# One GpSimd instruction of the front moved: the BatchNorm power behind the second norm shift

## The chip, the cores and the metric

The kernel runs on one core of one Trainium2 chip. The metric is the device time of one execution in microseconds. A core has five engines that run their own instruction streams in program order and wait for each other by semaphores: TensorE (PE, matmul), VectorE (DVE), ScalarE (ACT), GpSimd (POOL) and SyncE (SP, which here only issues DMAs).

## The reference, cut to what matters

The input x has 8 images of 512 channels and 32 x 32 points, all in float32. One block is computed:

- a GroupNorm of x with 32 groups of 16 channels each (mean and variance over the 16 channels and all points, then (x - mean) / sqrt(var + 1e-5));
- cv1, a 1x1 convolution 512 to 512, then BatchNorm with given statistics and SiLU; its output is cut into two halves of 256 channels, y0 and y1;
- two bottlenecks in a row on y1, each a 3x3 convolution with BatchNorm and SiLU, an attention of 4 heads over the 1024 points, a 1x1 convolution with BatchNorm and SiLU, and a residual;
- cv2, a 1x1 convolution over the 1024 channels of y0, y1 and the two bottleneck outputs, with BatchNorm and SiLU, added to x.

What the change touches is the front of this:

```python
x = x + layer(gn(x))                          # gn: GroupNorm
s = g / jnp.sqrt(v + BN_EPS)                  # BatchNorm factor of every convolution
cbs = silu((conv(x, w) - m) * s + b)          # conv, BatchNorm, SiLU
```

## The kernel before, in words

The eight images are worked off in four pairs. Before the first pair stands a front, in which everything that later stages take for granted is made for the first time: the images are loaded, the filters of the 3x3 convolution are transformed (`make_u`, on DVE with a few copies on ACT), the BatchNorm factors of all layers are made, image 0 and image 1 are normalised, and cv1 is computed for both. From about 78 us on PE works on the 3x3 convolution of the first pair.

An image is four tiles of 128 channels by 1024 points (`x` for image 0, `x_second` for image 1). The GroupNorm of some of these tiles is `group_norm_part` (L820). Its steps are:

- statistics per channel, on DVE (L770, L771) or, for tiles named in `by_act`, on ACT (L811 to L818);
- means over the groups by a small matmul with a constant matrix (`gm_ps`, L777), then the deviations on DVE (L786 to L789: `gm` is the negative mean, `dev` the variance), then a second small matmul (`gv_ps`, L777) and `gr = gv_ps + eps` on DVE (L796);
- on POOL `gr = gr ** -0.5` (L797) and `shift = gm * gr` (L833);
- on ACT `x = gr * x + shift`, half a tile at a time (L839).

Image 0 is done in two parts: its tiles 0 and 1 first, its tiles 2 and 3 as a second part of the same function. Image 1 is a third call, with all four tiles.

The BatchNorm factors need `rstd = (var + eps) ** -0.5` for 16 columns: `nc.vector.tensor_scalar` adds the epsilon (L2131), POOL takes the power (L2132), and later DVE makes the scale `sh` and the bias `bh` out of it (L2139 to L2144). They are read first by the first SiLU of cv1 (L523, on ACT).

cv1 of an image is, for each of 4 output tiles, a sum over 4 input tiles (k) and 2 halves. A float32 matmul of 512 columns shows as two rows in the trace. In the front the sums are begun with the tiles that are normalised first: before the second norm part is there, PE works on k = 0 and 1 of three output tiles (`begin`, 24 rows); then it goes on with k = 2 and 3 (L551, 32 rows), until the small matmul `gm_ps` of image 1 stands in its stream; then half an output tile, `gv_ps`, the last half, and then image 1 (64 rows).

The order on each engine is the order in which the tile scheduler emits instructions. `tc.issue_after(ins)` puts an instruction behind another one in that order; engines wait only for what they read or overwrite. POOL issues DMAs too: the stores of the transformed filters (L481) stand in the same stream behind the shifts.

Of the kernel before, what the change touches and what calls it, by code (L numbers as in the profile page):

```python
# [62 lines left out]
def kernel(  # L63
# [1965 lines left out]
    s = stages(act, small, ps_big, ps_av, 6)  # L2029
# [71 lines left out]
    with tc.issue_after(loaded.ins), tc.issue_after(averaged.ins):  # L2101
        for _ in range(5):
            made = next(chunk)
# [17 lines left out]
    with tc.issue_after(averaged.ins):  # L2121
        made = next(chunk)
# [3 lines left out]
    with tc.issue_after(first.ins), tc.issue_after(made.ins):  # L2126
        multiplied, _, applied, powered = next(norm)
    with tc.issue_after(multiplied.ins):
        begin(Y_ORDER[2], range(NX // 2))
    with tc.issue_after(made.ins), tc.issue_after(powered.ins):  # L2130
        nc.vector.tensor_scalar(rstd, bnp[:, :, 3], BN_EPS, None, ALU.add)  # L2131
        scaled = nc.gpsimd.tensor_tensor(rstd, rstd, mhalf[:, :NBN], ALU.pow)  # L2132
        for _ in range(4):
            made = next(chunk)
    with tc.issue_after(made.ins):
# [2 lines left out]
    with tc.issue_after(made.ins):  # L2138
# [4 lines left out]
        for at in bn_m1:  # L2143
            made = nc.vector.tensor_scalar(sh[:, at : at + NM], sh[:, at : at + NM], 1 / 36, None, ALU.mult)  # L2144
# [17 lines left out]
    with tc.issue_after(made.ins):  # L2162
        for _ in range(2):
            made = next(chunk)
# [3 lines left out]
    for steps, times in ((other, 2), (chunk, 3)):  # L2168
        with tc.issue_after(made.ins):
            for _ in range(times):  # L2170
                made = next(steps)
# [10 lines left out]
    multiplied, read, applied, powered = second["norm"]  # L2182
    shifted = s.shift_made[0]
    copies_behind[0] = applied
    with tc.issue_after(read.ins):
        for _ in range(2):
            made = next(chunk)
# [777 lines left out]
```

## Time and profile before

| what | value |
|---|---|
| time, median of 3 runs | 2205.9 us (2205.38 to 2206.28) |
| the profiled execution's own time | 2206.06 us |
| its span, first to last instruction | 2204.5 us |
| mean granted TensorE clock | 0.998 of full speed |
| PE busy | 2176.4 us, 99% of the span |
| DVE busy | 1814.6 us, 82% |
| ACT busy | 1094.6 us, 50% |
| POOL busy | 216.9 us, 10% |

A row of the timeline gives the start, the time from there to the end of the last instruction in it, the engine, the line, what is written from what, how many instructions are merged in it, and in brackets how long the engine had sat idle before it and what ended that. Matmul ends are modelled. A row of a waits view gives who waited for whom, the total, how often, and the longest. A row of a windows view gives a stretch, its length, the busy time of each engine with its count of instructions, the granted clock and the DMA load.

### The profile page before, as it was taken

The page shows a single profiled execution, that of the slowest core. Times are in us where ns is not written, and L with a number is a line of the kernel's source. Part 1 is how long each engine was busy: PE and PEld are TensorE (multiplying, and loading weights), DVE is VectorE, ACT ScalarE, POOL GpSimd, SP SyncE. Part 2 cuts the span into 40 slices and gives each one's busy share as a digit, 9 for nine tenths or more (in the row PEclk, how much of TensorE's full clock was granted, in tenths as well). Part 3 has the DMA queues.
Part 4 walks back from the last instruction along what each step waited for, and adds up shares of the span by engine and source line. Part 5 has one row for each costly group of instructions (what it writes and reads, how often), then busy time and mean ns, then how long its engine had stood idle before and what let it go on. Part 6 is the DMA issues. An engine that isn't in the chain of part 4 may idle for free.

```text
span 2204.5 us, 41005 instructions
## 1 busy us (share of the span) xinstructions
PE 2176.4 (99%) x16546; PEld 1121.3 (51%) x16546; DVE 1814.6 (82%) x3002; ACT 1094.6 (50%) x1320; POOL 216.9 (10%) x387
## 2 busy tenths in 40 slices
PE   7999999999999999999999999999999999999998
PEld 3653437343484444734458443564346734383445
DVE  7988879878978688986898868997798877897676
ACT  6555553554225666356314676456522465336543
POOL 3322210000210000000022000000002100000001
PEclk9999999999999999999999999999999999999999
DMA  6954547212583323612159141543126811261224
GB/s 220 338 173 130 181 132 279 83 49 78 143 284 107 104 99 120 214 50 77 56 137 328 35 161 42 180 144 103 33 68 176 295 30 45 92 207 36 68 59 116
DMA packets 133129, 290.75 MB, mean 132 GB/s; under 512 B 33636, under 2 KB 58976, under 8 KB 131908
## 3 DMA queue, kind: packets, MB, share of 16 engines
q1 hardware_dynamic: 101908, 200.62, 27.5%
q0 software_dynamic: 31024, 87.44, 13.2%
q8 instruction: 132, 2.16, 0.4%
q14 instruction: 65, 0.53, 0.1%
HBM read 218.40 MB, written 69.60 MB: 131 GB/s over the span
## 4 chain that ended last, share of the span: by engine, by line
PE 95%; DVE 3%; issue 1%; DMA 1%; ACT 0%; SPq 0%; POOL 0%; DVEq 0%; ACTq 0%; POOLq 0%
PE av_ps L1138 19%; PE l_ps L1101 19%; PE c_ps L689 11%; PE p_ps L975 8%; PE c L1375 6%; PE m_ps L1355 5%; PE ps L551 5%; PE c_q L1423 5%; PE x_ps L1847 4%; PE p_ps L981 3%; PE c L1407 3%; PE c_new L1375 2%; PE s_ps L1156 1%; DVE acc L1122 1%; PE p_ps L937 1%
## 5 line engine op out<-in xcount | busy, mean ns | idle before, releaser
L1105 ACT ACTIVATE pt<-l_ps 128x1024 f32<-128x1024 f32 x512 | 495.9, 1023 | 332.5 <-PE l_ps L1101 256.1
L1138 PE MATMUL av_ps<-pt,vT 64*64 64x512 f32 x4096 | 484.9, 590 | 0.8 <-DVE z L1146 0.8
L1101 PE MATMUL l_ps<-q,kr 64*64 64x512 f32 x4096 | 485.2, 590 | 0.0
L1122 DVE TENSOR_TENSOR acc<-acc,pt 128x1024 f32<-128x1024 f32 x362 | 442.8, 1223 | 37.2 <-ACT pt L1105 9.4
L1138 PEld LDWEIGHTS av_ps<-pt,vT 64*64 64x64 f32 x4096 | 157.5, 133 | 278.3 <-issue 234.5
L1101 PEld LDWEIGHTS l_ps<-q,kr 64*64 64x64 f32 x4096 | 158.4, 133 | 267.9 <-issue 245.2
L689 PE MATMUL c_ps<-v_in,u 128*64 128x128 f32 x4320 | 238.4, 273 | 0.3
L689 PEld LDWEIGHTS c_ps<-v_in,u 128*64 128x64 f32 x4320 | 235.7, 137 | 5.2 <-issue 5.2
L1146 DVE TENSOR_TENSOR z<-av_ps,z 128x512 f32<-128x512 f32 x64 | 44.0, 688 | 97.5 <-ACT z L1145 97.3
L1355 PE MATMUL m_ps<-z,m_sb 128*128 128x512 f32 x256 | 114.1, 593 | 0.0
L975 PE MATMUL p_ps<-t_z,sq 128*128 128x512 f32 x224 | 105.9, 595 | 0.0
L694 ACT COPY c_m<-c_ps 128x512 f32<-128x512 f32 x48 | 28.1, 585 | 150.5 <-PE c_ps L689 131.5
L1119 DVE TENSOR_TENSOR acc<-pt 128x1024 f32<-128x1024 f32 x64 | 78.1, 1221 | 14.2 <-PE s_ps L1156 9.2
L523 ACT ACTIVATE t<-m_ps,bh,sh 128x512 f32<-128x512 f32 x64 | 46.3, 773 | 86.5 <-PE m_ps L1355 85.3
L975 PE MATMUL p_ps<-z,sq 128*128 128x512 f32 x168 | 81.3, 604 | 0.2
L1355 PEld LDWEIGHTS m_ps<-z,m_sb 128*128 128x128 f32 x256 | 47.7, 190 | 56.8 <-issue 51.4
L1523 POOL DMA_DIRECT2D c_out<-in_x_dram x48 | 43.5, 1049 | 294.7 <-ACT c_out L523 292.1
L1214 DVE TENSOR_TENSOR z<-z,rs 128x512 f32<-128x512 f32 x64 | 42.4, 687 | 33.3 <-DMA rs<-r_dram 33.2
L523 ACT ACTIVATE z<-z,bh,sh 128x512 f32<-128x512 f32 x64 | 48.8, 811 | 22.9 <-DVE z L754 22.9
L975 PEld LDWEIGHTS p_ps<-t_z,sq 128*128 128x128 f32 x224 | 39.5, 191 | 36.5 <-issue 34.4
L523 ACT ACTIVATE c_out<-c,bh,sh 128x512 f32<-128x512 f32 x12 | 14.0, 1278 | 85.7 <-PE c L1407 77.7
L1847 PE MATMUL x_ps<-t_x,sw 128*128 128x512 f32 x128 | 55.9, 592 | 0.0
(410 smaller groups left out, 3342.0 us busy)
## 6 DMA issues: line engine op xcount, KB each, us to landing
u<-u SPq DMA_DIRECT2D x135, 512.0 KB
y_in<-y SPq DMA_DIRECT2D x32, 512.0 KB
rs<-r_dram SPq DMA_DIRECT2D x126, 128.0 KB
sq<-sq SPq DMA_DIRECT2D x42, 384.0 KB
x<-in_x_dram SPq DMA_DIRECT2D x28, 512.0 KB
r_in<-r SPq DMA_DIRECT2D x28, 512.0 KB
c_out<-in_x_dram POOLq DMA_DIRECT2D x56, 256.0 KB, 6.6
out_dram<-c_out POOLq DMA_DIRECT2D x56, 256.0 KB, 5.2
```

Of the source, the lines that this page charges most:

```text
L523: silued[0] = nc.scalar.activation(dst, src, AF.Silu, scale=sh[:, k : k + 1], bias=bh[:, k : k + 1])
L551: last_product[0] = nc.tensor.matmul(ps[:, half, :], w_of(k), rhs_of(k, half), start=(k == begin), stop=(k == end))
L689: conv_product[0] = nc.tensor.matmul(to[o], us[cp][:, k, row, c, o], rhs, start=(k == 0), stop=(k == NM - 1),)
L975: nc.tensor.matmul(ps[:, o, :], w[:, o, :], rhs, start=not onto, stop=True, skip_group_check=onto)
L1101: nc.tensor.matmul(ps[kh * HD : (kh + 1) * HD, hd, :], kr[r, c, o : o + HD], q[r, c, ts(half, HALF)], start=True, stop=True,)
L1105: last_exp[0] = exp = nc.scalar.activation(pt, ps, AF.Exp, scale=SCALE)
L1122: ins = nc.vector.tensor_tensor(accs[g], accs[g], pt[i], ALU.add)
L1138: nc.tensor.matmul(avs[g][hd * HD : (hd + 1) * HD, kh, :], vT[r, j, o : o + HD], pt[i][r, hd, :], start=(j == 0), stop=(j == NJ - 1),)
L1355: nc.tensor.matmul(pss[half][:, oc, :], m2_sb[:, n, k, ts(oc, P)], ao[:, k, ts(half, HALF)], start=(k == 0), stop=(k == NM - 1),)
L1375: nc.tensor.matmul(ps[:, o, :], w[:, k, ts(o, P)], rhs[part][:, c], start=(k == 0 and not onto), stop=(k == KB - 1), skip_group_check=onto,)
L1423: nc.tensor.matmul(to, a[:, c], b[:, c], start=first and c == 0, stop=last and c == 1, skip_group_check=True)
L1847: nc.tensor.matmul(ps[:, o, :], w[:, c, ts(o, P)], rhs[c], start=(c == 0 and not onto), stop=(c == 1), skip_group_check=onto,)
```

## The change

The power of the BatchNorm factors is one POOL instruction of 128 x 16 elements. Before, it was ordered behind `powered`, the power of the second norm part of image 0, and so came between that power and the shift that is made from it. Now it is ordered behind that shift. Nothing else is changed; what is computed is the same.

```diff
     with tc.issue_after(made.ins), tc.issue_after(powered.ins):
         nc.vector.tensor_scalar(rstd, bnp[:, :, 3], BN_EPS, None, ALU.add)
+    with tc.issue_after(made.ins), tc.issue_after(s.shift_made[0].ins):
         scaled = nc.gpsimd.tensor_tensor(rstd, rstd, mhalf[:, :NBN], ALU.pow)
+    with tc.issue_after(made.ins), tc.issue_after(powered.ins):
         for _ in range(4):
             made = next(chunk)
```

Three instructions in a row on POOL, in the front: the power `gr_331` and the shift `shift_334` of the second norm part of image 0, and the power `rstd_135` of the BatchNorm factors. Before:

```order
L797 TENSOR_TENSOR gr_241<-gr_241,mhalf_126 128x2
L833 TENSOR_TENSOR shift_244<-gm_232,gr_241 128x2
L797 TENSOR_TENSOR gr_331<-gr_331,mhalf_126 128x2
L2132 TENSOR_TENSOR rstd_135<-rstd_135,mhalf_126 128x16
L833 TENSOR_TENSOR shift_334<-gm_310,gr_331 128x2
L481 DMA u0120_151<-u_new_408 128x512
L481 DMA u0121_152<-u_new_408 128x512
```

With the change, at the same place (its line is now L2133):

```order
L797 TENSOR_TENSOR gr_241<-gr_241,mhalf_126 128x2
L833 TENSOR_TENSOR shift_244<-gm_232,gr_241 128x2
L797 TENSOR_TENSOR gr_331<-gr_331,mhalf_126 128x2
L833 TENSOR_TENSOR shift_334<-gm_310,gr_331 128x2
L2133 TENSOR_TENSOR rstd_135<-rstd_135,mhalf_126 128x16
L481 DMA u0120_151<-u_new_408 128x512
L481 DMA u0121_152<-u_new_408 128x512
```

The power of 16 columns and the shift of 2 columns have changed places; the stores of the filters follow as before. On PE, DVE, ACT and SP no instruction stands at another place.

## The prediction

> **What bounds the kernel now.** I read the page first, then the waits of PE, then the timelines of the engines in the front.
>
> ```profile
> span 2204.5 us, 41005 instructions
> PE 2176.4 (99%) x16546; PEld 1121.3 (51%) x16546; DVE 1814.6 (82%) x3002; ACT 1094.6 (50%) x1320; POOL 216.9 (10%) x387
> PE ps L551 <- ACT x L839: 5.8, 2, 3.1
> PE ps L551 <- ACT x_second L839: 0.9, 1, 0.9
> ```
>
> PE is busy 99% of the span. What delays it can be counted on one hand, and a good part stands in the front: matmuls of cv1 (L551) that wait for ACT to normalise their input (L839), once 3.1 us, once 0.9. The timeline of PE gives the places.
>
> ```profile
> 22.18 3.70 PE L551 MATMUL ps<-x,w_cols 128*128 128x512 f32 x8
> 29.03 15.70 PE L551 MATMUL ps<-x,w_cols 128*128 128x512 f32 x32 [3.15 <-ACT x L839]
> 44.66 0.28 PE L777 MATMUL gm_ps<-mv,gmat 64*64 64x4 f32 x4
> 44.87 1.98 PE L551 MATMUL ps<-x,w_cols 128*128 128x512 f32 x4
> 46.78 0.28 PE L777 MATMUL gv_ps<-dev,gmat 64*64 64x4 f32 x4
> 46.99 1.98 PE L551 MATMUL ps<-x,w_cols 128*128 128x512 f32 x4
> 49.83 27.73 PE L551 MATMUL ps<-x_second,w_cols 128*128 128x512 f32 x64 [0.85 <-ACT x_second L839]
> ```
>
> PE stands still from 25.88 to 29.03. The 64 rows at 49.83 take 27.73 us, 0.433 us each; the 32 at 29.03 take 15.63 to the next start instead of 13.9. The granted clock says why:
>
> ```profile
> 30.40:33.80 3.40, 3.40 (x6) 1.30 (x4) 3.33 (x14) 3.40 (x6) 0.00 (x0) 0.51 0.02 8
> 33.80:36.00 2.20, 2.20 (x7) 1.00 (x6) 2.20 (x7) 2.17 (x7) 1.08 (x2) 0.99 0.22 88
> ```
>
> For 3.4 us after the pause PE runs at 0.51 of its clock, which costs about 1.7 us more. What ACT waits for stands on POOL:
>
> ```profile
> 9.93 0.83 POOL L797 TENSOR_TENSOR gr<-gr,mhalf 128x2 f32<-128x2 f32 x1 [7.04 <-DVE gr L796]
> 10.84 0.54 POOL L833 TENSOR_TENSOR shift<-gm,gr 128x2 f32<-128x2 f32 x1
> 22.54 0.70 POOL L797 TENSOR_TENSOR gr<-gr,mhalf 128x2 f32<-128x2 f32 x1 [11.16 <-DVE gr L796]
> 23.20 3.12 POOL L2132 TENSOR_TENSOR rstd<-rstd,mhalf 128x16 f32<-128x16 f32 x1
> 26.29 1.84 POOL L833 TENSOR_TENSOR shift<-gm,gr 128x2 f32<-128x2 f32 x1
> 28.07 0.74 POOL L481 DMA_DIRECT2D u<-u_new  x1
> 48.71 0.22 POOL L833 TENSOR_TENSOR shift<-gm,gr 128x4 f32<-128x4 f32 x1
> 11.41 2.93 ACT L839 ACTIVATE x<-x,shift,gr 128x512 f32<-128x512 f32 x4 [1.97 <-POOL shift L833]
> 28.16 2.93 ACT L839 ACTIVATE x<-x,shift,gr 128x512 f32<-128x512 f32 x4 [5.60 <-POOL shift L833]
> ```
>
> The first norm part of image 0 goes from the start of its power (9.93) to ACT (11.41) in 1.48 us. The second takes 5.62 (22.54 to 28.16), because the 16-column power lies between.
>
> **Step 1, ACT and the pause of PE.** Power and shift now follow each other as in the first part: ACT starts at 22.54 + 1.48 = 24.02, 4.14 us earlier. PE had its first matmul 0.87 us after ACT's start (29.03 less 28.16), so the data is there at 24.89, before PE is done with its 24 earlier rows at 25.88. ACT makes half a tile in 0.73 us (2.93 / 4), PE uses it in two rows, 0.87 us, so PE never catches up. The pause of 3.15 us goes, and with it what called up the low clock. The 32 rows end at 25.88 + 32 x 0.433 = 39.75, and `gm_ps` of image 1 could start there, 4.9 us earlier than 44.66.
>
> **Step 2, what is late next.** `gm_ps` also needs ACT's statistics of image 1, and behind it stands DVE.
>
> ```profile
> 31.00 1.04 ACT L811 ACTIVATE junk<-x_second 128x1024 f32<-128x1024 f32 x1
> 36.01 2.26 ACT L523 ACTIVATE ypad<-ps,bh,sh 128x512 f32<-128x512 f32 x2
> 42.68 0.21 ACT L818 ACTIVATE mv<-square 128x4 f32<-128x4 f32 x1
> 45.40 1.21 ACT L523 ACTIVATE y_half<-ps,bh,sh 128x512 f32<-128x512 f32 x1
> 48.96 2.93 ACT L839 ACTIVATE x_second<-x_second,shift,gr 128x512 f32<-128x512 f32 x4 [2.35 <-POOL shift L833]
> 26.59 0.28 DVE L447 TENSOR_SCALAR u_new<-ypad 128x256 f32<-128x256 f32 x1
> 31.19 0.18 DVE L2139 TENSOR_TENSOR sh<-bnp,rstd 128x16 f32<-128x16 f32 x1
> 31.72 0.23 DVE L2144 TENSOR_SCALAR sh<-sh 128x2 f32<-128x2 f32 x2
> 41.23 0.43 DVE L464 SCALAR_TENSOR_TENSOR u_new<-taps,u_new 128x256 f32<-128x256 f32 x1
> 44.98 0.16 DVE L786 TENSOR_SCALAR gm<-gm_ps 128x4 f32<-128x4 f32 x1 [3.33 <-PE gm_ps L777]
> 45.71 0.16 DVE L789 TENSOR_TENSOR dev<-dev,mv 128x4 f32<-128x4 f32 x1
> 47.11 0.16 DVE L796 TENSOR_SCALAR gr<-gv_ps 128x4 f32<-128x4 f32 x1 [0.76 <-PE gv_ps L777]
> DVE gm L786 <- PE gm_ps L777: 3.3, 1, 3.3
> DVE gr L796 <- PE gv_ps L777: 1.9, 2, 1.1
> ```
>
> ACT works without a gap from 28.16 to the end of its statistics at 42.89. Moved by 4.14 us, the first SiLU (36.01) comes to 31.87, where its `sh` is ready at 31.95 (end of L2144); a tenth is lost, and the statistics end at about 38.9, before PE needs them at 39.75.
>
> DVE does not move. From 22.30 on it transforms filters without a gap, until 41.66 (41.23 + 0.43), and only then reads `gm_ps`, in program order. In the trace it waits there 3.33 us and again 0.76 for `gv_ps`; the last two rows, the waits of DVE from 20 to 100 us, hold no other wait after that. So DVE can get nearer by 3.33 + 0.76 = 4.09 us and no more. Does it get all? `gm` starts at 41.65. `dev` ends 0.89 later (45.71 + 0.16 less 44.98), at 42.54. PE has by then done `gm_ps` and the 4 rows behind it (39.75 + 0.21 + 1.73 = 41.7), so `gv_ps` starts at about 42.7 and `gr` 0.33 later (47.11 less 46.78), at 43.02 instead of 47.11. That is all of it.
>
> **Step 3, from there on.** Power and shift of image 1 and ACT's L839 follow `gr` by the same times as before: ACT at 44.87 instead of 48.96 (the SiLU row at 45.40, ended at 46.61 before, ends at about 42.5), PE on image 1 at 45.74 instead of 49.83. PE is short of work for about 1.0 us before `gv_ps` and 1.1 before image 1, but these lie inside the 4.09. From 49.83 on PE is full, and DVE too: both streams move as they are. Later loads and stores are started by the same engines, so they move along.
>
> **Step 4, the instruction that is moved.** The 16-column power now starts at about 24 and ends 3.12 later at 27.1; if the shift's 1.84 us before was its tail (the shifts at 10.84 and 48.71 took 0.54 and 0.22), 1.3 to 1.6 later. DVE asks for it at 31.19, so at least 2.4 us cover it. The store L481, and what follows it on POOL, waits only for finished ACT work and moves from 28.07 to about 27.1.
>
> ```profile
> 24.00:26.00 2.00, 1.88 (x5) 0.57 (x3) 2.00 (x6) 0.00 (x0) 2.00 (x1) 1.00 1.03 408
> 28.00:30.00 2.00, 0.97 (x3) 0.49 (x4) 1.93 (x6) 1.84 (x3) 0.81 (x2) 1.00 1.16 348
> 30.00:32.00 2.00, 2.00 (x4) 0.81 (x3) 1.93 (x10) 2.00 (x4) 0.00 (x0) 0.61 0.17 63
> ```
>
> The DMA engines are full until 30 and then empty, so all tiles of image 1 are there by 30. ACT now asks for the first at 26.95 (24.02 + 2.93) rather than at 31.00. In the worst case it waits until 30, gains only 1.0, and the statistics end at 41.9: `gm` comes at 42.2, and 3.5 us of the gain are left. At 408 GB/s a tile of 512 KB takes 1.3 us and they come in order, ahead of other loads; I take nothing off.
>
> **The cushion.** `gm_ps` must start by 41.33 to be ready for DVE (0.32 us pass between 44.66 and 44.98). PE gets there if ACT starts by 41.33 - 13.87 - 0.87 = 26.59; ACT's own 14.73 us to its statistics give 26.6 too. Forecast is 24.02. A shift that again took 1.84 us, or anything else up to 2.5 us, would cost nothing.
>
> **The sum.** 2206.06 - 4.09 = 2201.97 for the profiled execution. Its 2206.06 is 0.16 over the median of the three runs, so 2201.8 us, 0.19% less. The three runs lie 0.9 us apart, so about 0.2% (4.4 us) is what a measurement here can tell from no change; the forecast stands just inside that.
>
> **Rivals.**
>
> *PE sets the gain, not DVE.* If the DVE work before `gm` is not the limit, 4.9 us come through: 2201.0 on the median. Against it speaks that DVE's order is unchanged and gap-free up to 41.66. 5%.
>
> *VectorE locks the shift out.* The 1.84 us of the shift lie beside DVE instructions with two SBUF inputs, as its new place does; the next one with a single input is L447 at 26.59. If the shift gets through only there, ACT starts at 26.59 + 0.54 = 27.1, 0.5 us past the cushion: gain 3.5, or, if PE's pause of 2.1 us again brings the low clock (1.7), about 1.9. 2202.4 to 2204.0. Against: the power at 22.54 and the shift at 10.84 ran beside such instructions without that. 5%. [...]
>
> *The low clock comes back later.* The two short pauses of PE (1.0 and 1.1 us) at 41.7 and 44.6 lie close together. If they call up 3.4 us at half clock from 45.74 on, 1.7 us are lost: gain 2.4, 2203.5. Before, only the 3.15 us pause was followed by a low clock, the 0.85 us one was not (its 64 rows ran at 0.433). 5%. [...]
>
> *Slower: the BatchNorm power starves.* Should POOL get the 16-column power done only once DVE itself stops for it at 31.19, DVE stands for 3.12 + 1.84 = 4.96 us: more than the 4.09 gained, so +0.9, 2206.8. It decides from a power that ends after 31.19 + 4.09 = 35.3. Against: at 23.20 it ran its 3.12 us in the thick of DVE's work. 3%, of which 2 over +0.2%.
>
> *Nothing moves the end,* 2205.9, if what is saved is lost again to transfers after 50 us: 2%.
>
> **How the numbers follow.** The forecast has 80%; scatter of some 0.4 us in the medians puts a quarter of that, 20, past 4.4 us. With 5 from the first rival that is 0.25 faster; 0.02 slower; 0.73 within 0.2%. The range runs from the first rival's 2201.0 less 0.2 of scatter, 2200.8, to the low-clock case plus 0.2, 2203.7.
>
> **What would show it.** Right: the shift starts near 23.3 and ACT's second L839 near 24; no pause of PE around 26 to 29, clock 1.0 from 26 to 36; `gm_ps` near 39.8, DVE's `gm` near 41.6 without a wait; image 1 on PE near 45.7; the rest in unchanged spacing, 4.1 us earlier. Wrong: a shift that ends after 26.6, a wait of DVE at `sh`, ACT waiting for a DMA at its statistics of image 1, a clock below 1.0 after 41, or a distance to before that shrinks after 50 us.

## The result, and the profile after

| what | before | after |
|---|---|---|
| time, median | 2205.28 us (2204.16 to 2206.51, 20 runs) | 2201.85 us (2200.69 to 2202.81, 20 runs) |
| ratio, 95% interval | | 0.9985 (0.9978 to 0.9991) |
| the profiled execution's own time | 2206.06 us | 2202.51 us |
| its span | 2204.5 us | 2201.0 us |

The change makes the kernel 3.4 us faster, 0.15%; the interval runs from 2.0 to 4.9 us. The forecast was 2201.8 us.

The timeline of POOL after, around the moved instruction:

```profile
22.50 0.70 POOL L797 TENSOR_TENSOR gr<-gr,mhalf 128x2 f32<-128x2 f32 x1 [11.15 <-DVE gr L796]
23.27 0.30 POOL L833 TENSOR_TENSOR shift<-gm,gr 128x2 f32<-128x2 f32 x1
23.53 3.08 POOL L2133 TENSOR_TENSOR rstd<-rstd,mhalf 128x16 f32<-128x16 f32 x1
26.57 0.74 POOL L481 DMA_DIRECT2D u<-u_new  x1
```

The shift stands directly behind its power and takes 0.30 us, and the 16-column power is over at 26.61. The timeline of ACT shows what this releases:

```profile
23.61 2.93 ACT L839 ACTIVATE x<-x,shift,gr 128x512 f32<-128x512 f32 x4 [1.12 <-POOL shift L833]
31.86 2.25 ACT L523 ACTIVATE ypad<-ps,bh,sh 128x512 f32<-128x512 f32 x2 [0.32 <-DVE bh L2143]
38.53 0.21 ACT L818 ACTIVATE mv<-square 128x4 f32<-128x4 f32 x1
44.73 2.93 ACT L839 ACTIVATE x_second<-x_second,shift,gr 128x512 f32<-128x512 f32 x4 [2.25 <-POOL shift L833]
```

ACT starts at 23.61 instead of 28.16. The first SiLU (31.86) waits 0.32 us for its bias, and there is no other idle time until the statistics of image 1 end at 38.74; a DMA is not waited for. The timeline of PE:

```profile
22.14 17.43 PE L551 MATMUL ps<-x,w_cols 128*128 128x512 f32 x40
39.50 0.28 PE L777 MATMUL gm_ps<-mv,gmat 64*64 64x4 f32 x4
42.57 0.28 PE L777 MATMUL gv_ps<-dev,gmat 64*64 64x4 f32 x4 [0.87 <-DVE dev L789]
45.60 27.73 PE L551 MATMUL ps<-x_second,w_cols 128*128 128x512 f32 x64 [0.84 <-ACT x_second L839]
```

The two pieces that the pause had separated, 8 rows and 32 rows, are now one row of 40 without a gap, 0.434 us each (from 22.14 to the next start at 39.50). The stretches of the windows view agree; the number after the five engines is the granted clock:

```profile
24.00:29.00 5.00, 5.00 (x13) 2.24 (x12) 4.96 (x14) 5.00 (x9) 3.31 (x2) 1.00 1.08 351
29.00:36.00 7.00, 7.00 (x18) 3.06 (x17) 6.90 (x24) 6.65 (x12) 1.08 (x2) 1.00 0.29 99
36.00:46.00 10.00, 8.29 (x26) 3.38 (x25) 9.72 (x31) 7.75 (x15) 2.78 (x5) 1.00 0.72 192
46.00:78.00 32.00, 32.00 (x148) 16.30 (x148) 31.34 (x72) 27.86 (x44) 15.53 (x34) 1.00 0.99 380
```

PE is full from 24 to 36 at a clock of 1.00, and the clock stays there. On DVE the group means of image 1 follow the last filter instruction without a bracket, that is without a wait, and so does `gr`:

```profile
41.20 0.42 DVE L464 SCALAR_TENSOR_TENSOR u_new<-taps,u_new 128x256 f32<-128x256 f32 x1
41.53 0.16 DVE L786 TENSOR_SCALAR gm<-gm_ps 128x4 f32<-128x4 f32 x1
...
42.89 0.16 DVE L796 TENSOR_SCALAR gr<-gv_ps 128x4 f32<-128x4 f32 x1
```

So image 1 comes to PE at 45.60 instead of 49.83, 4.23 us earlier. That distance holds for 2075 us: the last sums of the last attention (`s_ps`) come at 2120.72 after, at 2124.86 before. Behind them 0.6 us are given back in this pair of profiles. The last two scalings of DVE (L1214) wait for DMAs that spread the reciprocals of these sums to 128 partitions; before, and then after:

```profile
2135.94 0.69 DVE L1214 TENSOR_TENSOR z<-z,rs 128x512 f32<-128x512 f32 x1 [0.79 <-DMA rs<-r_dram]
2139.25 0.69 DVE L1214 TENSOR_TENSOR z<-z,rs 128x512 f32<-128x512 f32 x1 [2.62 <-DMA rs<-r_dram]
```

```profile
2131.37 0.69 DVE L1214 TENSOR_TENSOR z<-z,rs 128x512 f32<-128x512 f32 x1 [0.18 <-DMA rs<-r_dram]
2135.81 0.69 DVE L1214 TENSOR_TENSOR z<-z,rs 128x512 f32<-128x512 f32 x1 [3.75 <-DMA rs<-r_dram]
```

The second scaling comes 14.39 us after the last sums before (2139.25 less 2124.86), 15.09 after (2135.81 less 2120.72). From the spans: 4.23 less 0.09 of scatter in the middle less 0.64 at the end is 3.50, the difference of the two spans.

### The profile page after: what moved, and what is told of

It reads as the page before. It is cut to its first block, busy times and chain, and to the rows that moved or that the text cites. A ratio compares the mean times of both kernels' runs of the same rounds, so it can differ in the third digit from the quotient of the medians.

```text
span 2201.0 us, 41005 instructions
## 1 busy us (share of the span) xinstructions
PE 2174.9 (99%) x16546; PEld 1120.7 (51%) x16546; DVE 1814.1 (82%) x3002; ACT 1094.7 (50%) x1320; POOL 215.4 (10%) x387
## 4 chain that ended last, share of the span: by engine, by line
PE 94%; DVE 3%; issue 1%; DMA 1%; ACT 1%; POOL 0%; SPq 0%; DVEq 0%; ACTq 0%; POOLq 0%
PE av_ps L1138 20%; PE l_ps L1101 19%; PE c_ps L689 12%; PE p_ps L975 8%; PE c L1375 6%; PE ps L551 5%; PE m_ps L1355 5%; PE c_q L1423 5%; PE x_ps L1847 4%; PE p_ps L981 3%; PE c L1407 3%; PE c_new L1375 2%; PE s_ps L1156 1%; DVE acc L1122 1%; PE p_ps L937 1%
## 5 line engine op out<-in xcount | busy, mean ns | idle before, releaser
L1214 DVE TENSOR_TENSOR z<-z,rs 128x512 f32<-128x512 f32 x64 | 42.4, 686 | 32.2 <-DMA rs<-r_dram 32.1
```

## The experiments

The theory: POOL's order held up ACT and so PE; with that gone, DVE's program order caps the gain at the 4.09 us that DVE had stood waiting. The rivals: the gain is set by PE or ACT; the moved power or the shift is near a limit of its own; a part of the gain was never in every execution of the kernel before.

In the table, "distance" is what the change works on: the time on PE from the second small matmul of image 0's second norm part (`gv_ps`, at 21.97 before and 21.93 after) to the first matmul of image 1. "End" is the time from the start of the last `s_ps` to the end of the span. Each profile is one execution; the ratio is of medians, against the kernel before on the same chip.

| run | distance, us | end, us | median or time, us | ratio and interval |
|---|---|---|---|---|
| before | 27.86 | 79.64 | 2205.28 | |
| after | 23.67 | 80.28 | 2201.85 | 0.9985 (0.9978 to 0.9991) |
| again | 23.67 | 80.13 | 2201.94 | 0.9985 (0.9976 to 0.9995) |
| gm_early | 22.63 | 79.83 | 2201.36 | 0.9984 (0.9975 to 0.9993) |
| cushion | 23.68 | 79.74 | 2201.46 | 0.9984 (0.9975 to 0.9994) |
| rstd_late | 26.21 | 79.88 | 2204.54 | 0.9997 (0.9988 to 1.0007) |
| before_2, before_3, before_4 | 27.86, 26.16, 27.85 | 79.66, 80.38, 79.88 | 2204.91, 2204.90, 2205.94 | |
| warm | 26.16 | 79.51 | 2203.93 | 0.9995 (0.9986 to 1.0004) |
| tail | 23.67 | 90.85 | 2212.16 | 1.0032 (1.0020 to 1.0045) |
| gm_split | 22.95 | 79.95 | 2201.21 | 0.9983 (0.9974 to 0.9992) |
| best | 22.95 | 90.90 | 2212.10 | 1.0031 (1.0019 to 1.0044) |

The first four experiments ran beside 33 runs of the kernel before (2205.13 us), the before and warm group beside 15 (2205.16), the last three beside 17 (2205.35).

### again: the changed kernel once more

No edit.

> The changed kernel once more, unchanged. In the first profiles the front gained 4.1 us (PE on image 1, and every stage up to 2120 us), and 0.65 us of it were missing at the end, where DVE waits for the second pair of spread transfers of the last attention. Theory 'end scatter': that loss belongs to the landing of these transfers and differs from execution to execution; the front again gains 4.1 to 4.2, the end loses between 0 and 1, time 3 to 4.2 us under before. Rival 'the gain is given back': the end loses the same 0.65 every time.

Measured: 2201.94 us, 3.2 us under the kernel before on that chip, with the same distance to a hundredth, which a third profile with this front (tail) has too. So what lies between 3.2 and 4.2 is elsewhere. The end is 80.13 us, 0.49 more than in the first profile of before; two profiles could not tell scatter from a loss by the change, but the column of the table can: 79.51 to 80.38 us with POOL's old order and 79.74 to 80.28 with the new one, leaving out tail and best.

### gm_early: is it DVE's order that caps the gain?

The group means of image 1 and the power of them are put ahead of the last four filter instructions of a step on DVE.

```diff
-    chunk = make_u(0, 1, 0, ..., summed=False, aside=second_rstd)
+    chunk = make_u(0, 1, 0, ..., summed=False, aside=lambda first: first)
...
-    for steps, times in ((other, 2), (chunk, 3)):
+    for steps, times in ((other, 2), (chunk, 2)):
...
-    with tc.issue_after(averaged.ins):
-        next(chunk)
+    second_rstd(averaged)
+    with tc.issue_after(second["norm"][1].ins):
+        for _ in range(2):
+            next(chunk)
```

> The changed kernel, with the group means of image 1 (and the power behind them) put ahead of the last four DVE instructions of the filter step, which took 1.67 us. Theory 'DVE caps the front': DVE's read of the means moves from 41.5 to about 39.9, just behind PE's matmul for them at 39.5, PE starts image 1 about 1.1 us earlier, near 44.5, and the time falls by 0.6 to 1.1 us against the changed kernel (DVE itself ends its filters about 1 us later, which may take some of it back at the convolution). Rival 'ACT or PE caps it': PE starts image 1 at 45.6 as before and the time does not move.

Measured: the distance falls by 1.04 us, to 22.63. So the order on DVE is what caps the changed kernel, and neither PE nor ACT. But the median follows by 0.6 us only (2201.36 against 2201.94 of the changed kernel beside it, with intervals that overlap). The timelines of PE and of DVE say why:

```profile
45.10 27.73 PE L551 MATMUL ps<-x_second,w_cols 128*128 128x512 f32 x64 [0.73 <-ACT x_second L839]
```

```profile
42.50 0.16 DVE L796 TENSOR_SCALAR gr<-gv_ps 128x4 f32<-128x4 f32 x1 [1.01 <-PE gv_ps L777]
```

```profile
79.56 2.66 PE L689 MATMUL c_ps<-v_in,u_new 128*64 128x128 f32 x42 [0.77 <-DVE v_in L639]
```

DVE now stands 1.01 us for `gv_ps`, its remaining work ends that much later, and PE meets that 37 us further on, at the first convolution, where it waits 0.77 us. Behind that convolution's first part, where PE goes on with L551 (83.78 here, 83.81 in the changed kernel), 0.57 of the 1.04 us are left.

### cushion: can the shift be later at no cost?

A power of 8 columns that nobody reads is put between the power and the shift of image 0's second norm part (`bh` is overwritten later by its real values).

```diff
+            if by_act == NX // 2:
+                with tc.issue_after(powered[0].ins):
+                    spent = nc.gpsimd.tensor_tensor(bh[:, :8], ones[:, :8], mhalf[:, :8], ALU.pow)
+            with tc.issue_after(spent.ins) if by_act == NX // 2 else nullcontext():
-            shift_made[0] = nc.gpsimd.tensor_tensor(shift, gm, gr, ALU.mult)
+                shift_made[0] = nc.gpsimd.tensor_tensor(shift, gm, gr, ALU.mult)
```

> The changed kernel, with a power of 8 columns that nobody reads put between the power and the shift of the second norm part: ACT starts 1.4 to 1.9 us later, near 25.2. Theory 'cushion': PE's data is there at 26.1 instead of 25.85, its pause is 0.2 to 0.4 us and no low clock follows; the means of image 1 still wait for DVE at 41.5, the time does not move (within 0.3 us). Rival 'the shift sets the end one for one': 1.4 to 1.9 us slower than the changed kernel.

The timelines of POOL and of PE:

```profile
22.90 1.86 POOL L835 TENSOR_TENSOR bh<-ones,mhalf 128x8 f32<-128x8 f32 x1
24.73 0.20 POOL L837 TENSOR_TENSOR shift<-gm,gr 128x2 f32<-128x2 f32 x1
24.88 3.21 POOL L2137 TENSOR_TENSOR rstd<-rstd,mhalf 128x16 f32<-128x16 f32 x1
```

```profile
25.83 14.00 PE L551 MATMUL ps<-x,w_cols 128*128 128x512 f32 x32 [0.25 <-ACT x L843]
39.76 0.28 PE L777 MATMUL gm_ps<-mv,gmat 64*64 64x4 f32 x4
42.31 0.28 PE L777 MATMUL gv_ps<-dev,gmat 64*64 64x4 f32 x4 [0.36 <-DVE dev L789]
45.35 27.73 PE L551 MATMUL ps<-x_second,w_cols 128*128 128x512 f32 x64 [0.84 <-ACT x_second L843]
```

The shift comes 1.7 us later against `gv_ps` than in the changed kernel (24.73 less 21.67 is 3.06; 23.27 less 21.93 is 1.34). PE stands 0.25 us and waits 0.51 us less for `dev` (0.36 instead of 0.87), and the distance is 23.68. The delay costs nothing: it comes out of the time that PE would have waited for DVE.

### rstd_late: what if the moved power came too late for DVE?

Two powers of 16 columns that nobody reads are put ahead of the moved one.

```diff
-    with tc.issue_after(made.ins), tc.issue_after(s.shift_made[0].ins):
+    spent = s.shift_made[0]
+    for _ in range(2):
+        with tc.issue_after(made.ins), tc.issue_after(spent.ins):
+            spent = nc.gpsimd.tensor_tensor(bh, ones[:, :NBN], mhalf[:, :NBN], ALU.pow)
+    with tc.issue_after(made.ins), tc.issue_after(spent.ins):
         scaled = nc.gpsimd.tensor_tensor(rstd, rstd, mhalf[:, :NBN], ALU.pow)
```

> The changed kernel, with two powers of 16 columns that nobody reads put ahead of the power of the BatchNorm factors, behind the shift: that power ends about 6.2 us later, near 32.8, and DVE wants it at 31.15. Theory 'DVE caps the front': DVE waits about 1.7 us there, everything on DVE up to the means of image 1 is 1.7 later, and the time is 1.5 to 1.9 us above the changed kernel. Rival 'the BatchNorm factors are covered, PE sets the end': the first SiLU is late, but PE has work, and the time moves by under 0.5 us.

POOL's timeline, the waits of DVE between 20 and 100 us, and PE's timeline:

```profile
23.61 7.26 POOL L2135 TENSOR_TENSOR bh<-ones,mhalf 128x16 f32<-128x16 f32 x2
30.84 2.90 POOL L2137 TENSOR_TENSOR rstd<-rstd,mhalf 128x16 f32<-128x16 f32 x1
```

```profile
DVE sh L2145 <- POOL rstd L2137: 2.4, 1, 2.4
```

```profile
45.19 0.28 PE L777 MATMUL gv_ps<-dev,gmat 64*64 64x4 f32 x4 [1.73 <-DVE dev L789]
48.23 27.73 PE L551 MATMUL ps<-x_second,w_cols 128*128 128x512 f32 x64 [0.84 <-ACT x_second L839]
```

The power ends at 33.74, DVE stands 2.4 us for it, and the distance grows by 2.54 us, about one for one: from 22.3 on DVE has no slack before `gr`. The medians agree: 2204.54 against 2201.94 is 2.6 us. The expectation had put the dummy powers at 6.2 us and the wait at 1.7; they took 7.26, so the wait and the loss are larger than expected, and the mechanism is as expected.

### before_2, before_3, before_4: is the kernel before the same each time?

The kernel before, unchanged, three more profiled executions.

> The kernel before, once more, to see whether the low clock after its pause falls in every execution. The front's distance (from the gv matmul of the second norm part to PE's start on image 1) was 27.86 us in the first profile, with a low clock from 30.44 to 33.86, and 23.67 in both profiles of the changed kernel. Theory 'the low clock falls in some executions': the clock is looked at in steps of 3.41 us that stand anywhere against the pause, so some executions have no low clock and a distance of about 26.1; the gain then is 2.5 instead of 4.2 us. Rival 'always': 27.9 and a clock of 0.5 after the pause in each.

> As the run ahead: 27.9 us with the low clock, or about 26.1 without it. By the first theory a late end of the low clock at the start (past 17.5 us) goes with none after the pause.

> As the two runs ahead: 27.9 us with the low clock, or about 26.1 without it.

Measured: before_2 and before_4 are as the first profile, with 15.70 us for the 32 rows behind the pause and distances of 27.86 and 27.85. before_3 is not. Its timeline of PE, and a stretch of its windows view:

```profile
28.98 14.00 PE L551 MATMUL ps<-x,w_cols 128*128 128x512 f32 x32 [3.14 <-ACT x L839]
48.09 27.73 PE L551 MATMUL ps<-x_second,w_cols 128*128 128x512 f32 x64 [0.85 <-ACT x_second L839]
```

```profile
29.00:33.00 4.00, 4.00 (x10) 1.84 (x11) 3.90 (x16) 4.00 (x7) 0.00 (x0) 1.00 0.35 113
```

The pause is the same, 3.14 us, but the clock behind it is 1.00, and the 32 rows take 14.00 us. The distance is 26.16, 1.70 us less than in the other three. Against such an execution the change gains 26.16 less 23.67, 2.49 us, in the distance. The time of before_3 is not lower for it (2204.90 us, before_2 has 2204.91): its `gv_ps` came 0.77 us later than in before_2 (21.93 against 21.16) and its end is 0.72 us longer.

The trace also records when the granted clock changes. In the order of before, before_2, before_3 and before_4 it first rises to full at 16.79, 15.18, 16.83 and 16.26 us, and the low clock begins at 30.44, 28.84, never, and 29.92. That is 13.65 us after the rise, four times 3.41, and it lasts 3.41. (The expected sign, a rise past 17.5 us where no low clock follows, did not hold: the rise of before_3 is at 16.83.) So in these four executions the changes of the clock fit a grid of 3.41 us whose place differs from one execution to the next. The low clock at the very end of the span fits it too: in before it begins 2181.12 us after the first rise, 639 times 3.413, and in after 2177.70 us, 638 times 3.413. The stretch of the grid that ends where the low clock begins holds 2.00 us of the pause in before (29.03 less 27.03), 2.79 in before_2 (28.22 less 25.43) and 2.28 in before_4 (28.79 less 26.51). In before_3 the grid has a border at 27.07 and cuts the pause (25.84 to 28.98) into 1.23 and 1.91 us, and nothing follows. In these four executions, then, the border between low clock and none lies between 1.91 and 2.00 us idle in a stretch, with the modelled ends of the matmuls. The other nine traces, each laid on its own grid from the first rise on, do not contradict it: before PE's last matmul, the most idle stretch that no low clock followed has 1.84 us (in tail), and the low clock came back in tail and best alone, behind stretches idle for 2.51 us and more.

How often the low clock falls can be read from more than four executions. Each run has its mean granted clock on record, to three digits: 0.998 in the three profiles with the low clock, 0.999 in before_3. Of the 65 runs of the kernel before that stood beside the experiments, 43 have 0.998 and 22 have 0.999. It is a sign and not a proof, since the low clock at the very end of the span counts too (again has 0.998 with none in its front). In the three groups those with 0.999 are on average 0.4 to 0.8 us faster, not 1.70. The start may take back a part: in the four profiles `gv_ps` of image 0 comes at 21.16, 21.73, 21.97 and 21.93 us where the clock first rises at 15.18, 16.26, 16.79 and 16.83.

### warm: the low clock alone

The kernel before, with three matmuls that nobody reads (six rows) in PE's pause.

```diff
-        begin(Y_ORDER[2], range(NX // 2))
+        last_begun = begin(Y_ORDER[2], range(NX // 2))
+    warm = ps_av.tile([P, HALF], F32, tag="av", name="warm")
+    for n in range(3):
+        with tc.issue_after(last_begun.ins):
+            last_begun = nc.tensor.matmul(warm, w1_of(0, 0), xs[0][:, :HALF], start=n == 0, stop=n == 2)
```

> The kernel before, with three matmuls of 512 columns that nobody reads put into PE's pause of 3.15 us, so that the pause shrinks to about half a microsecond and no low clock follows. Theory 'the low clock falls in some executions': the front's distance is 26.1 us here (1.7 less than the first profile of before), and the time falls by 0.5 to 1.2 us against before, as much as the share of executions with a low clock times 1.7. Rival 'always': the time falls by 1.7. Rival 'the low clock costs nothing, ACT sets the distance': the time does not move.

```profile
24.95 2.74 PE L2133 MATMUL warm<-x,w_cols 128*128 128x512 f32 x6
28.26 14.00 PE L551 MATMUL ps<-x,w_cols 128*128 128x512 f32 x32 [0.57 <-ACT x L839]
```

ACT is as late as before, and PE is idle for 0.57 us instead of 3.15. No low clock follows, and the distance is 26.16, as in before_3. The median is 1.2 us under the kernel before on that chip (interval from 3.1 us faster to 0.9 us slower). So in this profile the low clock is gone with six rows that nobody reads in the pause; that this shortens the time is not shown, as the interval holds no change as well as the full 1.70 us. All 11 runs of warm have a mean clock of 0.999.

### tail: is the scatter at the end in how the transfers are issued?

The changed kernel; for the last attention one transfer per row of reciprocals instead of one per half of it.

```diff
                     rs = act.tile([P, HALF], F32, tag="rs", name="rs", bufs=4)
+                    if at + gs[-1] == NSUM - 1:
+                        spread_out[0] = nc.sync.dma_start(
+                            rs, r_dram[n].unsqueeze(1).to_broadcast([2, HD, HALF])
+                        )
+                        rss.append(rs)
+                        continue
                     for hd in range(2):
```

> The changed kernel, with one edit at the very end: the reciprocals of the last attention's sums are spread to 128 partitions by one transfer per row instead of two halves, so SyncE issues 2 transfers instead of 4 before VectorE's last scaling. If the scatter of the end (79.5 to 80.4 us from the last sums on PE to the end of the span, in ten profiles) is in how these transfers are issued and land, the second scaling of VectorE comes 0.5 to 1.2 us earlier (13.3 to 14.0 us after the last sums instead of 14.3 to 15.2) and the time falls by 0.3 to 0.8 us, to about 2201.3. If the landing is set by the bytes or by the trip of a transfer alone, nothing changes: 79.5 to 80.4 us, and 2201.9 on the median. The front is untouched: 23.67 us from the second group means of image 0 to image 1 on PE.

Measured: 10 us slower than the changed kernel, which neither side expected. DVE's timeline, and stretches of the windows view (the last two numbers are the mean load of the 16 DMA engines and GB/s):

```profile
2138.09 0.69 DVE L1220 TENSOR_TENSOR z<-z,rs 128x512 f32<-128x512 f32 x1 [7.91 <-DMA rs<-r_dram]
...
2144.60 0.69 DVE L1220 TENSOR_TENSOR z<-z,rs 128x512 f32<-128x512 f32 x1 [5.75 <-DMA rs<-r_dram]
```

```profile
2141.00:2143.00 2.00, 2.00 (x4) 0.65 (x3) 0.00 (x0) 0.00 (x0) 0.00 (x0) 0.61 0.13 52
2143.00:2145.00 2.00, 0.51 (x2) 0.00 (x0) 0.40 (x1) 1.45 (x2) 0.00 (x0) 1.00 0.06 25
```

SyncE issues for 1.13 us instead of 2.38, as meant. But the second scaling comes 24.65 us after the last sums (2144.60 less 2119.95) instead of 14.3 to 15.2. While DVE waits for the end of it, the DMA engines carry a mean load of 0.13 and then 0.06: about two and then one of sixteen at work, worked out as 16 x 0.13 and 16 x 0.06. The packets in the trace say the same: both kernels spread the reciprocals in 256 packets of 2 KB, of which at most 3 are under way at once here and up to 18 in the changed kernel. Each of the two new transfers has the two halves of a row as its outer dimension, where each of the four in the changed kernel has 64 partitions; that this is what lowers the load is the author's reading, and no run shows it. The clock of 0.61 is the low clock again: it begins at 2135.74, within PE's wait of 5.60 us for the first scaling, and ends at 2142.57. PE is done at 2143.51 with what that scaling released, before the second one at 2144.60, so the low clock does not hold this up. What makes the end scatter by 0.9 us stays open. In the eleven profiles without this edit the last half of the spread packets runs beside 256 packets of 2 KB from POOL's queue, which begin 10.0 to 10.4 us after the last sums; whether that makes them scatter was not tried.

### gm_split: gm_early without its new wait

The same as gm_early, but `gr` of image 1 is put two filter instructions later on DVE (`make_u` takes a step `midway` that is called behind its L457), so that DVE works while PE makes `gv_ps`.

```diff
-    chunk = make_u(0, 1, 0, ..., summed=False, aside=second_rstd)
+    chunk = make_u(0, 1, 0, ..., summed=False, aside=lambda first: first, midway=second_rstd)
...
                 first = last = stt(g0, g2, 4.0, g0, ALU.mult, ALU.add)
+                if midway:
+                    last = midway(first)
...
-    for steps, times in ((other, 2), (chunk, 3)):
+    for steps, times in ((other, 2), (chunk, 2)):
...
-        next(chunk)
+        for _ in range(2):
+            next(chunk)
```

> As in gm_early, VectorE makes image 1's group means ahead of its last filter instructions, but the last of these steps (the one that waits for the second small matmul) is put one filter step later, so that VectorE need not stand 1.1 us for it. If VectorE's program order was what capped the gain at 4.1 us, and what gm_early lost again (0.77 us before the first convolution) was that wait handed on, the distance is 22.6 us again, VectorE waits for at most 0.4 us, the wait before the first convolution falls to 0.3 us or less, and the time is 0.5 to 1.0 us under the changed kernel: 2201.0 to 2201.4. If the wait before the first convolution is there because VectorE is now the fuller engine over the whole front, it stays at 0.6 us or more and the time is that of gm_early or of the changed kernel, 2201.4 to 2201.9.

```profile
41.57 0.16 DVE L798 TENSOR_SCALAR gr<-gv_ps 128x4 f32<-128x4 f32 x1 [0.23 <-PE gv_ps L779]
```

```profile
44.49 27.73 PE L553 MATMUL ps<-x_second,w_cols 128*128 128x512 f32 x64 [1.05 <-ACT x_second L841]
```

DVE waits 0.23 us instead of 1.01, and the wait before the first convolution is gone. The distance is 22.95, 0.72 less than in the changed kernel, and all of that is left where PE goes on with L553 at 82.70. It is 0.3 more than in gm_early, because this time the shift of image 1 took 0.56 us on POOL instead of 0.23. The time is 2201.21 us, the lowest of all, with a ratio of 0.9983 where the changed kernel has 0.9985; the intervals overlap, so that it beats the changed kernel is read from the profiles rather than from the times. From `gv_ps` to the last sums it takes 2098.01 us, gm_early 2098.10, the changed kernel 2098.79 and 2099.08; so its lead over gm_early is small.

### best: gm_split and tail together

Both edits.

> Both edits together, gm_split and tail. If each brings its part and they are independent, as they stand 2000 us apart, the gains add up: 0.8 to 1.8 us under the changed kernel, 2200.1 to 2201.1 us. If neither does, 2201.9.

Measured: 2212.10 us. It has gm_split's front (distance 22.95) and tail's end (90.90), and its span is 0.6 us under that of tail, while the medians lie 0.06 apart. In the profiles the parts add up as expected, but one of them is a loss, so the expected 2200.1 to 2201.1 is missed by 11 us, and it is no best version. By the profiles gm_split is.

## Why the prediction was right, point by point

**Step 1, ACT and the pause of PE.** Right. ACT started 0.4 us earlier than forecast, because power and shift took 1.11 us to ACT's start and not 1.48. The pause is gone, the clock is 1.00, and `gm_ps` starts at 39.50 (39.75 forecast).

**Step 2, what is late next.** Right: `gm` at 41.53 (41.65), `gv_ps` at 42.57 (42.7), `gr` at 42.89 (43.02), without a wait on DVE. gm_early shows that it is DVE's order that sets this: with that changed, image 1 comes 1.04 us earlier. rstd_late shows it from the other side, since a delay of DVE is passed on one for one.

**Step 3, from there on.** Image 1 came at 45.60 (45.74). The front gave 4.23 us, 4.09 were forecast, and nothing of it was lost up to 2120 us. That the whole rest moves along held up to the last attention; there the landing of four transfers scatters. The second scaling of DVE came between 14.31 and 15.17 us after the last sums in the eleven profiles that leave the transfers as they are, before and after alike (14.39 and 15.17 in two profiles of before). So the 0.6 us lost there in this pair of profiles are not the change's doing.

**Step 4, the instruction that is moved.** The power ended at 26.61 (27.1 forecast, or 1.3 to 1.6 later), 4.5 us ahead of its reader (DVE at 31.15). The later end did not come. Whether the shift's 1.84 us before were a tail of the power stays open: behind the 8-column power of cushion the shift takes 0.20, which speaks against it, but no run has a shift behind a 16-column power at another place.

**The transfers of image 1.** No wait, as taken; the statistics ended at 38.74 (38.9).

**The cushion.** Shown by cushion: 1.7 us of its 2.5 used, nothing lost.

**The sum.** This is the step with a term of the wrong size. The 4.09 us are right against the profile that they were worked out from, and the median moved by 3.4 (3.2 in the second comparison; the interval of the first, 2.0 to 4.9, holds 4.09). The prediction took the low clock behind the pause, "about 1.7 us more", as part of every execution. It measures 1.70, but before_3 has the same pause without it: three of four profiles have it. Against an execution with it the distance shrinks by 4.19, against one without it by 2.49. If the grid lies anywhere with equal chance, a pause of 3.15 us escapes where a border cuts it so that neither part is over 1.95 (between the 1.91 and the 2.00 of these executions), which is 0.75 of 3.41 us, or 22 in 100; the mean gain would be 2.49 + 0.78 x 1.70 = 3.8, an estimate from the rows of the four executions. With the share of 43 in 65 that the recorded clocks point to, it would be 2.49 + 0.66 x 1.70 = 3.6, an estimate too. A gain of 3.4 would be had with about half ((3.4 - 2.49) / 1.70 = 0.54). The medians are too coarse to tell these apart, and warm's 1.2 us (0.7 of 1.70) lies between. So the low clock's share is the likely cause of what is missing, and not a measured one. The offset to the median had the same flaw: 0.16 was taken from three runs, and the profiled execution lies 0.8 us over the median of twenty. That the end came out at 2201.85 and the forecast at 2201.8 is therefore partly luck, since the two errors cancel: 0.7 us less gained, from a start 0.6 us lower.

**The rivals.** *PE sets the gain:* no, DVE does. *VectorE locks the shift out:* no. The shift took 0.30 us at its new place (23.27), beside DVE instructions with two inputs (L455 at 22.97, L459 at 23.44), and 0.20 in cushion beside DVE's filter work. *The low clock comes back later:* no. The pauses of 0.87 and 0.84 us are followed by 32 us at 1.00. They, and the other short ones of this kernel, leave a stretch of the grid idle for less than the 1.91 us that no low clock followed in before_3. *The BatchNorm power starves:* no, but its price is now measured by rstd_late, 2.54 us for a power that ends at 33.74, close to the 33.74 - 31.19 = 2.55 that the prediction's condition gives. *Nothing moves the end:* no.

## What to carry to other kernels

When an instruction is moved out of a chain, work out the gain from the engine that is next in line: the sum of that engine's waits there is a cap, and here it was met to 0.1 us. The low clock was in three of four profiles of the kernel before, and the end scattered by 0.9 us in eleven; such a term belongs into the sum with the share of executions that have it, read from several profiles of the kernel before or from the mean clock recorded with each run. And an instruction that waits belongs behind work that could be done meanwhile: gm_early gained 1.04 us and lost about half of it again in a wait 37 us later, gm_split kept its 0.72.

## What the runs showed of the hardware that was not expected

- The low clock does not follow from the length of the pause alone: 3.15 us was followed by 3.4 us at half clock in three executions of the kernel before, and 3.14 us by none in the fourth. What fits these four is a grid of 3.41 us: the low clock followed a stretch idle for 2.00 to 2.79 us, and none followed one idle for 1.91. Pauses of 0.25 to 1.73 us between 22 and 50 us were not followed by it in any profile here.
- The shift of 128 x 2 took 1.84 us on POOL behind a 16-column power, 0.30 to 0.54 behind a 2-column one and 0.20 behind an 8-column one; up to 50 us a power took 0.70 to 0.83 us for 2 columns, 1.14 to 1.27 for 4, 1.86 for 8 and 2.9 to 3.6 for 16.
- Two transfers that spread one row each to 128 partitions landed 9.5 to 10.3 us later than four that spread half a row each to 64, at the same bytes (the scaling behind them came 24.65 us after the last sums against 14.31 to 15.17).
